# Which slot a tile gets, and the order of the steps of a layer's first chunk and of the convolution, in a one-core RWKV and graph-convolution kernel

## The chip, the cores and the metric

The kernel runs on one core of a Trainium2 chip. The metric is the device time of one execution in microseconds (us); lower is better. Five engines work side by side, each through its own list of instructions in order: PE (TensorE, matrix products into PSUM), DVE (VectorE), ACT (ScalarE), POOL (GpSimd), and SP, which here only issues DMAs. A semaphore makes an instruction wait for another engine; everything behind it in its list waits with it.

## The reference, cut to what matters

The input is x, 16 images of 192 channels by 56 by 56 positions (T = 3136). Three WKV layers, each added to its input, are followed by one graph convolution, also added.

```
per WKV layer:  xs = groupnorm(x) as [T, C];  k, v, r = xs Wk', xs Wv', xs Wr'
   forward  y_t = (p + e^(u+k_t) v_t) / (q + e^(u+k_t));  p <- e^w p + e^k v;  q <- e^w q + e^k
   backward the same from the other end;  h = sigmoid(r) * (y_fwd + y_bwd) / 2
   h = layernorm over channels(h);  x = x + h Wo'
convolution:  xn = groupnorm(x);  xj = max(0, the four shifts of xn by 2 rows or columns - xn)
   x = x + gelu([xn, xj] W' + b)
```

## The kernel before, in words

**Tiling.** Two images make a pair (8 pairs). A pair's 192 channels lie as three planes j = 0, 1, 2 of 128 partitions (plane 1 holds the last 64 channels of both images); `ORDER` is (0, 2, 1). T is cut into 7 chunks of L = 448 positions. A chunk's tile is 128 x 3 x 448 float32, a **slot**: there are 33 (`NSLOTS`), and `free` lists the free ones. `Slot(what)` takes the first of the list, `give()` puts one at its end. A slot's new writer waits for its old readers.

**Work per chunk.** A forward unit "A" (functions `a_*`): product k, exp (ek), product v, `a_ekv` (DVE, ekv = v ek), prefix scans `a_q` of ek and `a_p` of ekv (`scan`, DVE, three planes each), `a_den` and `a_num` (`bonus`, DVE), `invert` (ACT: Ln, then Exp of its negative), `a_y` (POOL, y = num times 1/den). `save` copies a scan's last column to the next chunk's tile. A backward unit "B" (`b_*`) runs the chunks from 6 to 0: product r (`b_gate`) and `b_exp`, scans `b_q` and `b_p`, `b_den`, `invert`, `b_num`, `b_sigmoid` (ACT), and `b_mix` (POOL, three operations per plane, nine in all: ekv times 1/den; added to the forward y; times the sigmoid). Then the layernorm: `b_squares` (ACT), `b_sums` (PE), `b_rs1` (ACT), `b_rs2` (PE), `b_rs3` (ACT), `b_spread` (PE, broadcast of 1/std, tile rsb), `b_scale` (DVE), product `b_out`, `b_x` (DVE, residual; wrapped by `add`, followed by a DMA to DRAM), and `b_stats` (ACT, sums for the next groupnorm, wrapped by `sum_up`). A convolution unit "C": product with half 0 of the weights (`c_product(a, 0)`), the maxima `c_rows` and `c_columns` (DVE), product with half 1, `c_gelu` (ACT, with a table load on each side), `c_add` (POOL), and `store` (DMA to the output).

**Steps.** Nothing is scheduled by a planner: under `manual_schedule` each engine's list is the order in which Python calls the operations. A list of 249 steps pairs the backward unit of one pair of images with a forward or convolution unit of another. `both_a_first` is the step of chunk A0 of a layer beside B5 (17 of them, each behind `backward_alone`), `both_a` the other steps of B and A (85), `both_c` those of B and C (42, in 7 groups of six; B runs from 5 to 0 and C from 0 to 5), `forward_a` an A alone (66), `forward_c` a C alone. `late` holds for each unfinished B how far its layernorm has come: of_stage(0) is the B of the step before, whose layernorm runs in this step; `gap()` runs one part of the groupnorm of a layer that is about to begin (`norm_sums`, `norm_var`, `norm_fold`, `norm_fold_r`). PSUM has seven banks for products (`banks` takes three, `release` gives them back).

**The two parts that change.** In `both_a_first` the order around the scan is

```
        a_q(*a) ... keys(nfront)
        a_p(*a, V)                 # the scan of ekv, then the save by DVE
        spread_and_scale(l)        # b_spread, b_scale, b_out of the B before
        ... a_den(*a); ln(den()); add(l); a_num(*a); exp_minus(den()); a_y(*a)
```

In `both_c`, inside a group, DVE's list is b_den, add, c_rows, c_columns, b_num, then the next B's b_q and b_p, then b_scale; PE's is gate r, cv half 0, sums, b_rs2, cv half 1, spread, out; ACT's is exp of r, squares, Ln, rs1, Exp, six statistics, rs3, sigmoid, gelu; POOL's is nine of b_mix, the save of p, c_add.

Of the kernel before, what the change touches and what calls it, by code (L numbers as in the profile page):

```python
# [473 lines left out]
def fast_path(ctx: ExitStack, tc: tile.TileContext, flag, x, wproj, wfold, wcfold, wconst, wgroup, sums, picks, vecs, out):  # L474
# [24 lines left out]

    free = [f"slot{i}" for i in range(NSLOTS)]  # L500

    class Slot:
        def __init__(self, what):
            self.tag = free.pop(0)
            rows = keep.tile([P, 3, L + 4], F32, tag=self.tag, name=name(what))
            self.full, self.lead = rows[:, :, 2 : L + 3], rows[:, :, 1 : L + 2]
            self.t = rows[:, :, 2 : L + 2]

        def give(self):
            free.append(self.tag)  # L510

# [347 lines left out]
    def scan(run, key, data, step, first):  # L859

        dec = params[run.l][0]
        s = Slot(key)
        for j in ORDER:
            if first:
                out, e = s.t[:, j, ::step], data.t[:, j, ::step]
            elif step > 0:
                out, e = s.lead[:, j, :], data.lead[:, j, :]
            else:
                out, e = s.full[:, j, ::-1], data.full[:, j, ::-1]
            V.tensor_tensor_scan(  # L870
                out, dec[:, column(j)].to_broadcast([P, L if first else L + 1]), e, 0.0, ALU.mult, ALU.add
            )
        return s
# [15 lines left out]

    def slot_of(slots, c, what):  # L890
        if c not in slots:
            slots[c] = Slot(what)
        return slots[c]
# [8 lines left out]
    def a_keys(run, c):  # L902
        if not once(run, "k", c):
            return
        product(run, "k", run.w[0], run.xa[c], c == 0)
        slot_of(run.ek, c, "ek")
        if c == 0:
            take_bias(run, "k", S)
# [42 lines left out]
    def a_p(run, c, eng=G):  # L951
        run.h[c] = scan(run, "p", run.ekv[c], AHEAD, c == 0)
        if c < NL - 1:
            save(run.h[c], AHEAD, slot_of(run.ekv, c + 1, "ekv"), eng)

# [19 lines left out]
    def a_y(run, c):  # L975
        den = run.den.pop(c)
        G.tensor_mul(run.h[c].t, run.h[c].t, den.t)  # L977
        den.give()

# [27 lines left out]
    def b_den(run, c):  # L1007
        q = run.q.pop(c)
        bonus(run, run.ek[c], run.ek[c], q)
        q.give()  # L1010

# [6 lines left out]
    def b_num(run, c):  # L1018
        p = run.p.pop(c)
        bonus(run, run.ekv[c], run.ekv[c], p)  # L1020
        p.give()

    def b_mix(run, c):
        y, h, sg, den = run.ekv.pop(c), run.h[c], run.sg.pop(c), run.ek[c]
        for j in ORDER:
            G.tensor_mul(y.t[:, j, :], y.t[:, j, :], den.t[:, j, :])  # L1026
            G.tensor_add(h.t[:, j, :], h.t[:, j, :], y.t[:, j, :])  # L1027
            G.tensor_mul(h.t[:, j, :], h.t[:, j, :], sg.t[:, j, :])  # L1028
        y.give()
        sg.give()  # L1030

# [5 lines left out]
    def b_sums(run, c):  # L1037
# [5 lines left out]
        for n, (t, i) in enumerate(parts):  # L1043
            PE.matmul(st[32 * n : 32 * n + 32, :L], ones[:, 1 + i, :], t[:, 1, :], start=False, stop=n < 2)  # L1044
        sq.give()

# [27 lines left out]
    def b_out(run, c):  # L1074
        h = run.h.pop(c)
        run.ps["o"] = banks("ops")
        project(run.ps["o"], params[run.l][5], of(h.t), L)
        h.give()

# [294 lines left out]
    def both_a_first(b, a, nback, nfront, loads):  # L1374
# [13 lines left out]
        b_mix(*b)  # L1388
        slot_of(a[0].ekv, a[1] + 1, "ekv")
        for u in loads:  # L1390
# [12 lines left out]
        keys(nfront)  # L1403
        a_p(*a, V)
        spread_and_scale(l)
# [6 lines left out]
        b_rs1(*b)  # L1412
        ln(den())
        add(l)
        a_num(*a)
        late[b] = 0.5
        exp_minus(den())
        a_y(*a)

    def both_c(b, a, nback, nfront, loads):  # L1420

        l0, l1, l2 = of_stage(0), of_stage(1), of_stage(2)
        load_ahead(nback)
        first = nback is not None and not l1
        b_q(*b)
        b_p(*b)
        if first:

            b_gate(*nback[1:])
            b_exp(*nback[1:])  # L1430
            c_product(*a, 0)
        if l0:
            squares_and_sums(l0)
        b_den(*b)
        ln(b[0].ek[b[1]])
        if l0:
            b_rs1(*l0)
        exp_minus(b[0].ek[b[1]])
        if l2:
            add(l2)  # L1440
            sum_up()
        if l1:
            spread_and_scale(l1)
        gap()
        store()
        for u in loads:
            load_ahead(u)
        if nback is not None:
            if not first:
                b_gate(*nback[1:])  # L1450
                b_exp(*nback[1:])
        else:
            keys(nfront)
            exp_keys(nfront)
        if not first:
# [12 lines left out]
        b_mix(*b)  # L1468
        if l1:
            add(l1)  # L1470
            sum_up()
        if nback is not None:
            b_q(*nback[1:])
            b_p(*nback[1:])
        ahead = nback is None and l0 and nfront is not None and nfront[0] == "A"
        if ahead:
            a_q(*nfront[1:])
            a_save(*nfront[1:])
            b_spread(*l0)
            c_end(*a, False)  # L1480
            a_values(*nfront[1:])
            b_scale(*l0)
            b_out(*l0)
            late[l0] = 2
        elif l0:
            spread_and_scale(l0)
        if not ahead:
            c_end(*a, False)
        late[b] = 0
# [201 lines left out]
    with tc.manual_schedule(engines={PE.engine, V.engine, S.engine, G.engine, nc.sync.engine}):  # L1691
# [46 lines left out]
        store()  # L1738
        assert not late and not unsummed and not convs

# [99 lines left out]
```

## Time and profile before

| what | us |
|---|---|
| median of 3 runs (5244.23 to 5249.13) | 5248.44 |
| profiled execution, its own time | 5246.37 |
| its span, from the first to the last instruction | 5244.4 |
| DVE busy (92%) | 4837.0 |
| PE busy (90%) | 4701.2 |
| ACT busy (70%) | 3680.4 |
| POOL busy (55%) | 2900.0 |
| mean granted PE clock | 0.943 |

A profile's row gives line, engine, operation, tiles out<-in, count, then busy time, mean ns of one, and the engine's idle time just before with what ended it. A timeline row gives start, duration, engine, line, operation and, in brackets, the idle time before and its releaser. Tile names are those of the code with numbers left out: in the rows of `b_mix` tile p is the forward y. "Busy" on DVE and POOL includes time in which an instruction has begun and is held up. A matmul's end is modelled, so PE's busy share is no measure of how near it is to its peak.

### The profile page before, as it was taken

The numbers are of one execution on the slowest core, as the hardware profiler recorded it, in microseconds if no ns is written. First come the engines' busy times: TensorE is split into PE (matmuls) and PEld (weight loads), VectorE is DVE, ScalarE is ACT, GpSimd is POOL, SyncE is SP. The second block draws the span as 40 slices with busy tenths as digits, with TensorE's granted clock in tenths as the row PEclk, the third lists the DMA queues.
The fourth block names the chain that finished last, engine by engine and source line by source line (L and its number), as shares of the span: only waits on it lengthen the run. The fifth ranks groups of instructions, "written<-read, shape, count | busy, mean of one in ns | idle before, by whom it ended". The sixth has DMA issues, their size and how long they took to land. (4 is left out here: it accounts for less than half of the span.)

```text
span 5244.4 us, 51899 instructions
## 1 busy us (share of the span) xinstructions
PE 4701.2 (90%) x15542; PEld 1493.0 (28%) x15542; DVE 4837.0 (92%) x6288; ACT 3680.4 (70%) x7163; POOL 2900.0 (55%) x2234
## 2 busy tenths in 40 slices
PE   7999998989899998898989999889898999999887
PEld 3222222223232222222323222222232322222222
DVE  6999889899999998999999999889999999999996
ACT  6777777776566777776656678778766667777672
POOL 1666555555455655555454556556545455666562
PEclk9999999999999999999999999999999999999998
DMA  5222222223232222223323223222332322222233
GB/s 153 69 82 82 95 82 92 85 90 116 89 116 71 87 90 88 85 85 100 118 79 113 84 74 100 87 78 93 115 100 87 111 74 76 75 83 81 73 108 114
DMA packets 314275, 482.47 MB, mean 92 GB/s; under 512 B 66432, under 2 KB 306688, under 8 KB 313984
## 3 DMA queue, kind: packets, MB, share of 16 engines
q1 hardware_dynamic: 312832, 477.59, 28.5%
q8 instruction: 125, 2.05, 0.2%
q10 hardware_dynamic: 1152, 1.48, 0.1%
q14 instruction: 166, 1.36, 0.1%
HBM read 324.83 MB, written 154.14 MB: 91 GB/s over the span
## 5 line engine op out<-in xcount | busy, mean ns | idle before, releaser
L870 DVE TENSOR_TENSOR_SCAN p<-fdecays,ekv 128x449 f32<-128x449 f32 (+1 forms) x1008 | 1021.9, 1069 | 113.8 <-POOL p L1027 60.1
L870 DVE TENSOR_TENSOR_SCAN q<-fdecays,ek 128x449 f32<-128x449 f32 (+1 forms) x1008 | 1024.7, 1072 | 8.9 <-ACT ek L915 8.8
L977 POOL TENSOR_TENSOR p<-p,q 128x1344 f32<-128x1344 f32 x168 | 511.6, 3045 | 838.2 <-ACT q L973 543.0
L1026 POOL TENSOR_TENSOR ekv<-ekv,ek 128x448 f32<-128x448 f32 x504 | 627.1, 1244 | 625.0 <-ACT ek L973 392.9
L1028 POOL TENSOR_TENSOR p<-p,sg 128x448 f32<-128x448 f32 x504 | 633.3, 1257 | 144.5 <-ACT ek L879 101.3
L1027 POOL TENSOR_TENSOR p<-p,ekv 128x448 f32<-128x448 f32 x504 | 600.9, 1192 | 39.5
L881 POOL COPY ekv<-p 128x3 f32<-128x3 f32 x265 | 221.8, 837 | 538.5 <-DVE p L870 531.5
L915 ACT ACTIVATE ek<-k,k 128x448 f32<-128x448 f32 x504 | 296.9, 633 | 213.1 <-PE k L596 168.1
L730 ACT ACTIVATE fjunk<-x 128x448 f32<-128x448 f32 x672 | 387.7, 577 | 39.4 <-DVE x L1084 13.0
L1035 ACT ACTIVATE ek<-p 128x448 f32<-128x448 f32 x504 | 279.4, 572 | 168.4 <-POOL p L1028 167.9
L1066 PE MATMUL rsb<-rs,fpicks 32*128 32x448 f32 (+1 forms) x1008 | 342.0, 602 | 46.8 <-ACT rs L1060 46.8
L991 ACT ACTIVATE sg<-r,r 128x448 f32<-128x448 f32 x504 | 313.1, 627 | 95.6 <-PE r L596 72.3
L885 DVE SCALAR_TENSOR_TENSOR ek<-ek,fcc,q 128x896 f32<-128x896 f32 x336 | 374.0, 1154 | 0.0
L1071 DVE TENSOR_TENSOR p<-p,rsb 128x448 f32<-128x448 f32 x504 | 281.7, 615 | 92.0 <-PE rsb L1066 92.0
L1084 DVE SCALAR_TENSOR_TENSOR x<-ops,fwob,x 128x448 f32<-128x448 f32 x504 | 315.6, 674 | 49.3 <-PE ops L596 30.2
L729 ACT ACTIVATE fjunk<-x 128x448 f32<-128x448 f32 x600 | 342.8, 571 | 11.4
L885 DVE SCALAR_TENSOR_TENSOR q<-ek,fcc,q 128x896 f32<-128x896 f32 x336 | 343.0, 1062 | 6.3 <-ACT cvb L949 4.6
L1050 ACT ACTIVATE rs<-st 64x448 f32<-64x448 f32 x168 | 90.2, 537 | 358.0 <-PE st L1044 358.0
L970 ACT ACTIVATE q<-q 128x1344 f32<-128x1344 f32 x168 | 221.7, 1319 | 162.1 <-DVE q L885 114.1
L593 PE MATMUL ops<-p,fwo 128*128 128x448 f32 x336 | 210.0, 713 | 139.6 <-DVE p L1071 139.3
L935 DVE SCALAR_TENSOR_TENSOR ekv<-v,v,ek 128x448 f32<-128x448 f32 x504 | 313.5, 676 | 11.9 <-PE v L602 5.7
L885 DVE SCALAR_TENSOR_TENSOR ekv<-ekv,fcc,p 128x896 f32<-128x896 f32 x336 | 322.2, 1000 | 0.0
(236 smaller groups left out, 11827.6 us busy)
## 6 DMA issues: line engine op xcount, KB each, us to landing
x<-xd SPq DMA_DIRECT2D x240, 672.0 KB, 5.2
xd<-x SPq DMA_DIRECT2D x168, 672.0 KB, 3.8
x<-in_x_dram SPq DMA_DIRECT2D x320, 224.0 KB, 4.1
x<-in_x_dram SPq DMA_DIRECT2D x320, 112.0 KB, 4.0
out_dram<-ml SPq DMA_DIRECT2D x112, 224.0 KB, 2.3
m<-xd SPq DMA_DIRECT2D x112, 168.0 KB, 4.8
wkv<-in_wfold_dram SPq DMA_DIRECT2D x24, 640.0 KB, 5.4
out_dram<-ml SPq DMA_DIRECT2D x112, 112.0 KB, 2.3
```

Source lines behind the costliest of these rows:

```text
L729: S.activation(junk, xt[:, j, :], AF.Identity, accum_out=stats[:, 0, j, c : c + 1])
L730: S.activation(junk, xt[:, j, :], AF.Square, accum_out=stats[:, 1, j, c : c + 1])
L870: V.tensor_tensor_scan(out, dec[:, column(j)].to_broadcast([P, L if first else L + 1]), e, 0.0, ALU.mult, ALU.add)
L885: by_channel(lambda js, i: V.scalar_tensor_tensor(dst.t[:, js, :], e.t[:, js, :], cc[:, i : i + 1], state.t[:, js, :], ALU.mult, ALU.add))
L935: V.scalar_tensor_tensor(e.t[:, j, :], ps[j][:, 0:L], b[:, j, :], run.ek[c].t[:, j, :], ALU.add, ALU.mult)
L977: G.tensor_mul(run.h[c].t, run.h[c].t, den.t)
L991: S.activation(sg.t[:, j, :], ps[j][:, 0:L], AF.Exp, bias=b[:, j, :], scale=-1.0, accum_out=run.chk[:, at : at + 1])
L1026: G.tensor_mul(y.t[:, j, :], y.t[:, j, :], den.t[:, j, :])
L1027: G.tensor_add(h.t[:, j, :], h.t[:, j, :], y.t[:, j, :])
L1028: G.tensor_mul(h.t[:, j, :], h.t[:, j, :], sg.t[:, j, :])
L1066: PE.matmul(ps[j][:, :L], pick[rows, j, :], rs[rows, :], start=True, stop=True)
L1084: V.scalar_tensor_tensor(xj, ps[j][:, 0:L], wob[:, column(j)], xj, ALU.add, ALU.add, accum_out=run.new[:, 0, j, c : c + 1] if c == 0 else ...
```

## The change

Three things are done, all by reordering or by choosing another buffer. No arithmetic operation is added or removed; one kind of small copy moves from DVE to POOL.

1. `free` keeps with each slot the engine that read it last. A taker may name an engine: it then gets a slot last read by that engine if there is one, else one not last read by DVE, else any. Scans name DVE, ek names PE, ekv names the engine of its save.
2. `both_a_first`: the save after `a_p` goes to POOL, its slot is no longer taken early, and `invert` and `a_num` come ahead of `add`.
3. `both_c`: `b_scale` comes ahead of the next B's scans, `add` ahead of `b_den`; `b_spread` follows `b_gate`; the second half of a chunk's convolution product, its gelu and `c_add` are done in the following step; `b_out` opens the following step; the statistics go between the squares; Ln and Exp stand together ahead of `b_rs1`; the three `gap()` calls stand after `b_rs3`, after `c_rows` and after `c_columns`. In the last step of a group the current chunk's second product is done in the step itself, beside the one carried over.

```diff
-    free = [f"slot{i}" for i in range(NSLOTS)]
+    free = [(f"slot{i}", None) for i in range(NSLOTS)]
     class Slot:
-        def __init__(self, what):
-            self.tag = free.pop(0)
+        def __init__(self, what, engine=None):
+            own = [slot for slot in free if engine is not None and slot[1] is engine]
+            slot = (own + [slot for slot in free if slot[1] is not V] + free)[0]
+            free.remove(slot)
+            self.tag = slot[0]
...
-        def give(self):
-            free.append(self.tag)
+        def give(self, engine=None):
+            free.append((self.tag, engine))
...
-        s = Slot(key)
+        s = Slot(key, V)                                  (scan)
-        slot_of(run.ek, c, "ek")
+        slot_of(run.ek, c, "ek", PE)                      (a_keys)
-            save(run.h[c], AHEAD, slot_of(run.ekv, c + 1, "ekv"), eng)
+            save(run.h[c], AHEAD, slot_of(run.ekv, c + 1, "ekv", eng), eng)
                  den.give(G); q.give(V); p.give(V); y.give(G); sg.give(G); sq.give(PE); h.give(PE)
both_a_first:
-        slot_of(a[0].ekv, a[1] + 1, "ekv")
...
-        a_p(*a, V)
+        a_p(*a)
...
-        ln(den())
+        late[b] = 0.5
+        invert(den())
+        a_num(*a)
         add(l)
-        a_num(*a)
-        late[b] = 0.5
-        exp_minus(den())
         a_y(*a)
+    half = []
both_c:
-        l0, l1, l2 = of_stage(0), of_stage(1), of_stage(2)
+        l0, l1 = of_stage(0), of_stage(1.5)
         load_ahead(nback)
         first = nback is not None and not l1
+        store()
         b_q(*b)
         b_p(*b)
+        if l1:
+            b_out(*l1)
         if first:
             b_gate(*nback[1:])
             b_exp(*nback[1:])
             c_product(*a, 0)
+        if half:
+            c_product(*half[0], 1)
         if l0:
-            squares_and_sums(l0)
+            b_squares(*l0, (0,))
+        sum_up()
+        if l0:
+            b_squares(*l0, (2, 1))
+            b_sums(*l0)
+        if l1:
+            add(l1)
         b_den(*b)
-        ln(b[0].ek[b[1]])
+        invert(b[0].ek[b[1]])
         if l0:
             b_rs1(*l0)
-        exp_minus(b[0].ek[b[1]])
-        if l2:
-            add(l2)
-            sum_up()
-        if l1:
-            spread_and_scale(l1)
+            b_rs2(*l0)
+            b_rs3(*l0)
         gap()
-        store()
+        if half:
+            u = half.pop()
+            c_gelu(*u, False)
+            c_add(*u)
         (loads; keys, or b_gate and b_exp where not first, as before)
+        if l0:
+            b_spread(*l0)
         if not first:
             c_product(*a, 0)
         c_rows(*a)
-        if l0:
-            b_rs2(*l0)
-            b_rs3(*l0)
-            late[l0] = 1
+        gap()
         c_columns(*a)
-        c_product(*a, 1)
-        gap()
         gap()
         b_num(*b)
         b_sigmoid(*b)
         b_mix(*b)
         if nback is not None:
+            if l0:
+                b_scale(*l0)
+                late[l0] = 1.5
             b_q(*nback[1:])
             b_p(*nback[1:])
-        (spread_and_scale(l0) and c_end(a), or with the next A's start between them)
+            half.append(a)
+        else:
+            (a_q and a_save of the next A where it is one; c_product(a, 1); c_end(a);
+             a_values of that A; b_scale(l0), b_out(l0), late[l0] = 2)
         late[b] = 0
```

More of the change, by code (lines that the diff above doesn't have):

```diff
@@ L861, in scan @@
         dec = params[run.l][0]
-        s = Slot(key)
+        s = Slot(key, V)
         for j in ORDER:
@@ L888, in fast_path, with slot_of @@
     AHEAD, BACK = 1, -1
-    def slot_of(slots, c, what):
+    def slot_of(slots, c, what, engine=None):
         if c not in slots:
-            slots[c] = Slot(what)
+            slots[c] = Slot(what, engine)
         return slots[c]
@@ L905, in a_keys @@
         product(run, "k", run.w[0], run.xa[c], c == 0)
-        slot_of(run.ek, c, "ek")
+        slot_of(run.ek, c, "ek", PE)
         if c == 0:
@@ L977, in a_y @@
         G.tensor_mul(run.h[c].t, run.h[c].t, den.t)
-        den.give()
+        den.give(G)
     def b_gate(run, c):
@@ L1009, in b_den @@
         bonus(run, run.ek[c], run.ek[c], q)
-        q.give()
+        q.give(V)
     def b_p(run, c):
@@ L1020, in b_num @@
         bonus(run, run.ekv[c], run.ekv[c], p)
-        p.give()
+        p.give(V)
     def b_mix(run, c):
@@ L1028, in b_mix @@
             G.tensor_mul(h.t[:, j, :], h.t[:, j, :], sg.t[:, j, :])
-        y.give()
-        sg.give()
+        y.give(G)
+        sg.give(G)
     def b_squares(run, c, js=ORDER):
@@ L1044, in b_sums @@
             PE.matmul(st[32 * n : 32 * n + 32, :L], ones[:, 1 + i, :], t[:, 1, :], start=False, stop=n < 2)
-        sq.give()
+        sq.give(PE)
     def b_rs1(run, c):
@@ L1077, in b_out @@
         project(run.ps["o"], params[run.l][5], of(h.t), L)
-        h.give()
+        h.give(PE)
     def b_x(run, c):
@@ L1431, in both_c @@
             c_product(*a, 0)
+        if half:
+            c_product(*half[0], 1)
         if l0:
-            squares_and_sums(l0)
+            b_squares(*l0, (0,))
[5 more added lines that the diff above has]
+            add(l1)
         b_den(*b)
-        ln(b[0].ek[b[1]])
+        invert(b[0].ek[b[1]])
         if l0:
             b_rs1(*l0)
-        exp_minus(b[0].ek[b[1]])
-        if l2:
-            add(l2)
-            sum_up()
-        if l1:
-            spread_and_scale(l1)
+            b_rs2(*l0)
+            b_rs3(*l0)
         gap()
-        store()
+        if half:
+            u = half.pop()
+            c_gelu(*u, False)
+            c_add(*u)
         for u in loads:
             load_ahead(u)
[L1448 to L1452, printed above, removed]
+        if nback is None:
             keys(nfront)
             exp_keys(nfront)
+        elif not first:
+            b_gate(*nback[1:])
+            b_exp(*nback[1:])
+        if l0:
+            b_spread(*l0)
         if not first:
@@ L1468, in both_c @@
         b_mix(*b)
-        if l1:
-            add(l1)
-            sum_up()
         if nback is not None:
+            if l0:
+                b_scale(*l0)
+                late[l0] = 1.5
             b_q(*nback[1:])
             b_p(*nback[1:])
[L1475 to L1479, printed above, removed]
-            c_end(*a, False)
[L1481 to L1488, printed above, removed]
+            half.append(a)
+        else:
+            ahead = nfront is not None and nfront[0] == "A"
+            if ahead:
+                a_q(*nfront[1:])
+                a_save(*nfront[1:])
+            c_product(*a, 1)
+            c_end(*a, False)
+            if ahead:
+                a_values(*nfront[1:])
+            if l0:
+                b_scale(*l0)
+                b_out(*l0)
+                late[l0] = 2
         late[b] = 0
@@ L1738, in fast_path @@
         store()
-        assert not late and not unsummed and not convs
+        assert not late and not unsummed and not convs and not half
     least = small.tile([P, 1], F32, tag="p2", name="fleast")
```

## The prediction

> **What bounds the kernel now.** I read the page's busy shares first, then who waited for whom on DVE, then time windows of single steps, then timelines inside them.
>
> ```profile
> PE 4701.2 (90%) x15542; PEld 1493.0 (28%) x15542; DVE 4837.0 (92%) x6288; ACT 3680.4 (70%) x7163; POOL 2900.0 (55%) x2234
> ...
> DVE p L1071 <- PE rsb L1066: 92.0, 54, 18.6
> DVE p L870 <- POOL p L1027: 60.1, 18, 6.8
> DVE p L870 <- POOL p L1028: 53.6, 6, 9.0
> DVE x L1084 <- PE ops L596: 30.2, 22, 4.4
> ```
>
> DVE and PE are both near full, so a wait of DVE costs time unless PE is behind as well. The second and third wait (columns: total, times, longest) are of a scan for POOL, and the data of that scan come from DVE itself. L1027 and L1028 are the last readers of two slots that `b_mix` frees: the scan waits for its output buffer, 113.7 us in 24 places.
>
> Windows of one step each (time, then busy of PE, PEld, DVE, ACT, POOL, granted clock), for one pair of layers with these waits and one without:
>
> ```profile
> 712.80:751.40 38.60, 34.09 (x119) 10.64 (x118) 26.05 (x35) 21.94 (x42) 18.85 (x16) 0.91 0.18 56
> ...
> 1645.60:1673.70 28.10, 27.44 (x107) 8.58 (x106) 26.28 (x35) 18.90 (x34) 17.90 (x15) 1.00 0.23 75
> ...
> 1721.80:1745.40 23.60, 23.30 (x82) 7.11 (x80) 23.60 (x30) 19.29 (x38) 15.22 (x12) 1.00 0.27 89
> ```
>
> The first two rows run from `both_a_first` to the step behind it: DVE's work is equal (26.1 and 26.3), the time is 38.6 against 28.1. The third is a `both_a` step without a wait: DVE full at 23.6, PE right behind it. Inside the slow one:
>
> ```profile
> 730.21 3.05 DVE L870 TENSOR_TENSOR_SCAN p<-fdecays,ekv 128x448 f32<-128x448 f32 x3 [8.95 <-POOL p L1028]
> 733.29 0.17 DVE L881 COPY ekv<-p 128x3 f32<-128x3 f32 x1
> ...
> 739.22 1.28 DVE L1084 SCALAR_TENSOR_TENSOR x<-ops,fwob,x 128x448 f32<-128x448 f32 x2 [2.52 <-PE ops L596]
> 741.55 0.69 DVE L1084 SCALAR_TENSOR_TENSOR x<-ops,fwob,x 128x448 f32<-128x448 f32 x1 [1.05 <-PE ops L602]
> ...
> 728.22 1.97 PE L1066 MATMUL rsb<-rs,fpicks 32*128 32x448 f32 x6
> ...
> 729.04 1.13 POOL L1028 TENSOR_TENSOR p<-p,sg 128x448 f32<-128x448 f32 x1
> ```
>
> The scan could start at 721.2; it starts when `b_mix` ends. What would stop DVE next is the PE row: rsb, which starts at 728.2.
>
> Convolution steps, by windows:
>
> ```profile
> 1138.30:1166.60 28.30, 23.85 (x86) 7.27 (x82) 27.27 (x31) 22.49 (x42) 16.09 (x11) 1.00 0.24 81
> 1166.60:1191.50 24.90, 24.10 (x80) 7.63 (x80) 24.83 (x32) 16.64 (x30) 15.76 (x11) 0.93 0.44 137
> 1191.50:1223.20 31.70, 29.03 (x105) 10.24 (x104) 28.08 (x42) 24.72 (x51) 16.05 (x11) 0.95 0.53 174
> ...
> 1159.29 3.42 POOL L1154 TENSOR_TENSOR ml<-ml,x 128x1344 f32<-128x1344 f32 x1
> ...
> 1159.70 3.04 DVE L1121 TENSOR_TENSOR ml<-x 128x16 f32<-128x16 f32 x1
> ```
>
> DVE looks full, but the last row is an operation on 16 elements (0.16 to 0.17 us elsewhere) that takes 3.04 us while `c_add` runs on POOL: some of DVE's busy time is being held up.
>
> **Part 1, slots.** By the rule of the change a forward scan gets the slot that `b_den` or `b_num` of the same step has just freed, last read by DVE itself, in all 102 steps of B and A. So all 24 waits go. What each is worth depends on what is late next.
> - Six first steps with about 9.0 us. By the timeline: scan 721.2 to 724.2; rsb's first plane is ready about 729.1, so DVE waits there 4.9; scaling to 730.8, a_den to 732.5, a_num to 734.2, add to 736.1. Before, the same work ended at 743.8. Gain 7.7, the reordering of part 2 included.
> - Three first steps with 6.8 (at 538): rsb comes at 537.7 there; the same sum ends at 544.5 instead of 549.95. Gain 5.5.
> - Fifteen later steps: the rest, 113.7 - 53.6 - 20.5 = 39.6. DVE is the bound there (PE's 22.7 us of work against 23.6), so I take it whole.
> - Waits on rsb that follow a slot wait one step later (2.0 and 0.6 us, in six groups, together 7.9): PE fell behind because `b_scale` came late. Gone too; bounds 0 and 7.9, I take 7.9.
>
> Sum: 6 x 7.7 + 3 x 5.5 + 39.6 + 7.9 = 110. The slots that other users get instead are a risk that the trace doesn't show: loads and `b_exp` could wait for `b_mix`. Bounds 0 and 9.0 us a step (the longest wait of this kind now); nothing lower, as a wait can't give time. I take 0, because those users write a step later and `b_mix` is done some 10 us before.
>
> **Part 2, the first step.** In the eight first steps without a slot wait `add` waits 0.26 + 0.59 for PE (at 1661.7); behind a_num it no longer does: 0.8 each, 6. The save moves to POOL: 0.42 us of DVE (x17, L881), hidden under the wait for rsb, against a POOL copy of 0.84 mean (x265, L881) between `b_mix` and `a_y`, where POOL idles 16 us (746.5). Both at nothing; without that cover 0.4 each way.
>
> **Part 3, the convolution.** I work out what one step needs on three paths, from uncontended rows.
> - PE: four products of 4.5 (r from 1179.34 to 1183.84), rsb 1.97, sums 1.75, rs2 0.96: 22.7.
> - DVE: scaling 1.6, scans 5.9, add 1.8, b_den 1.7, rows 1.6, columns 5.7, b_num 1.7: 20.0.
> - A loop through ACT and POOL, which the new order closes. From the last POOL operation of `b_mix`: last square 0.6, Ln and Exp 2.6, rs1 0.5, rs2 1.1, rs3 1.3, then gelu with its two table loads 4.5, three exps of r 2.1, sigmoid 2.7 (Ln at 1170.09, next free at 1172.8), and the seven `b_mix` operations that need the sigmoid, 8.2: 23.6. Before, gelu stood behind the sigmoid and was no part of such a loop.
>
> The shared port. The row above shows DVE held for the whole of `c_add`. The Trainium skill, SBUF — State Buffer, "Who interferes with whom", states why: a DVE instruction with two SBUF inputs and a GpSimd one that reads SBUF exclude each other for the whole instruction, while one SBUF input contends with nothing. By that rule scaling, scans and add (one input is PSUM) are free beside `b_mix`, and b_den, rows, columns, b_num are not. In the new order the nine operations of `b_mix` lie beside scaling, scans and add, 9.3 us; only b_den (two of 0.83) meets the last three. `c_add` comes 9.4 us behind the end of `b_mix`, when columns are over (they end at about 7). So the held-up time on DVE goes, but DVE no longer sets the step: POOL loses about 1.2 to b_den, and the loop becomes 23.6 + 1.2 = 24.8; I take 25.0.
>
> The clock. PE gets half its clock now and then: after the 2.2 us of waiting ahead of 1166.7 the window 1166.7 to 1170.1 shows 0.51 granted. The skill, TensorE: Matmul & The Clock Gate, "What's actually happening", says the clock halves after about 3.4 us of an idle window and a busy window releases it. By the trace shorter waits can do it. This speaks against the change: PE now waits for the sums (some 2 us) and for rs2 (1.5) in each step. By the rule neither halves it, PE stays at 22.7 and the loop at 25.0 holds; by the trace one window of 3.4 a step costs 1.7, PE 24.4, still under 25.0. The sum is the same; a second window would break it (below).
>
> Group by group: the first convolution step is as before up to the end of b5's mix (1128.4). Then four loops of 25.0, plus 3.0 where a groupnorm falls in (table scale 1.7 and rstd now ahead of the sigmoid; DVE's 3.3 of waiting for rstd moves behind c_rows), put the last mix's end at 1231.4. The last step carries two second products, 4.5 more on PE, and b_out of the one before: from 4.8 behind that end PE has k, rsb, cv, cv, v, 20.0, plus 1.0 for half clock: 1257.2 for the end of v, for which DVE waits. Now v ends at 1260.2. Gain 3 in six groups, and 5 in the last (no groupnorm, no v): 23. The new wait on v (about 5 us of DVE) is in this.
>
> SP: `store` moves to the head of the step, ahead of add's DMA; the four DMAs wait only for a `c_add` issued half a step earlier, and loads are a step ahead; 0, bounds 0 and 2.3 (a store's time to landing) a step for the one tile in six whose slot is written in that step.
>
> Sum: 110 + 6 + 23 = 139 off the profiled execution's 5246.4: 5107. The median lies 2.1 above that execution: **5110**. This kernel's measurement tells about 0.2% from no change.
>
> **The rivals.**
> - *Main case*, 0.50: 5110, own range 5070 to 5150.
> - *The convolution falls to PE's 22.7*: the loop is shorter than I think (the last three of `b_mix` not held up, table loads ahead of gelu's wait). For it: PE idle 0.1 to 0.9 us in two of the windows. Against: the loop's rows. 35 x 2.3 = 80 more: 5030. 0.20.
> - *The slot waits come back*: the fifteen later ones turn into waits on rsb, and half of the first steps' gain goes to half clock; convolution even. 5246.4 - 55 - 6 + 2 = 5187. For it: the 92.0 us on rsb and 0.91 clock in the slow window. Against: the window of 23.6. 0.21.
> - *Slower*: two waits of PE in each convolution step keep it at half clock through gate r and, a step on, out. Each takes 9.0 instead of 4.5, exps of r come 3.2 late, the addition and b_den follow; the loop is 29.5. 35 x 4.5 = 158 on top, less the 23: 5246.4 - 116 + 135 + 2 = 5267. It decides from a loop of about 29 us. Against: windows of half clock are mostly 3.4 or 6.8 now. 0.06.
> - *Even*, a loop near 28.5: 0.03.
>
> Faster by over 0.2% is the first three, 0.91; within 0.2% 0.03; slower 0.06. The range 5030 to 5190 reaches to both neighbours of the main case and leaves out the last two and part of the second.
>
> **What would show it.** No wait of L870 p on POOL; in first steps one on rsb of about 5 us in its place; `both_a` steps at 23.6 to 24.5 everywhere. Convolution steps near 25 each with DVE below 22 busy, no 3 us operation of 16 elements, POOL waiting for the sigmoid, ACT's list without long gaps; one wait on v at a group's end. Wrong it would be if the scans wait for something else, if `c_add` still lies beside columns, or if a convolution step is over 28 or under 23.

## The result, and the profile after

Eight runs of the changed kernel have a median of 5221.5 us (5199.0 to 5223.1), eight of the kernel before 5248.6 us (5242.4 to 5253.3): ratio 0.9945, interval 0.9936 to 0.9954. The change brings 27 to 29 us where the prediction had 139. The profiled execution took 5220.2 us, its span is 5218.2.

The page's row of busy times, then what DVE waited for (total, times, longest):

```profile
PE 4733.3 (91%) x15542; PEld 1498.8 (29%) x15542; DVE 4750.5 (91%) x6271; ACT 3684.6 (71%) x7163; POOL 2889.2 (55%) x2251
...
DVE p L1076 <- PE rsb L1071: 194.4, 96, 20.7
DVE nm L749 <- PE psg L607: 33.6, 14, 4.6
DVE v L862 <- PE v L601: 32.9, 6, 5.5
...
DVE q L875 <- ACT ek L920: 25.4, 7, 7.9
...
DVE v L862 <- PE v L607: 10.5, 7, 1.6
```

No scan waits for POOL any more: 113.7 us are gone as forecast. But the wait for rsb has grown from 92.0 us in 54 places to 194.4 in 96, and three small waits are new. (Lines stand five lower than before: L1071 for rsb is L1076 here for the scaling that waits, the scan is L875.)

Windows of single steps (time, then busy of PE, PEld, DVE, ACT, POOL, granted clock): a first step; a later step with statistics of the other pair's input (`count(z)`); one without them; then four steps of a convolution group, the third with the groupnorm:

```profile
711.80:741.60 29.80, 29.14 (x112) 8.86 (x110) 26.42 (x34) 20.46 (x39) 18.95 (x17) 1.00 0.14 47
794.90:822.20 27.30, 24.89 (x81) 7.62 (x80) 24.62 (x30) 20.45 (x42) 15.65 (x12) 0.94 0.23 77
1671.20:1694.80 23.60, 23.31 (x82) 7.12 (x82) 23.60 (x31) 19.29 (x38) 15.34 (x13) 1.00 0.28 89
1128.10:1151.20 23.10, 21.32 (x77) 6.78 (x78) 21.46 (x32) 17.47 (x33) 15.47 (x11) 1.00 0.41 135
1151.20:1175.60 24.40, 22.63 (x82) 7.07 (x80) 21.36 (x31) 18.76 (x35) 15.05 (x11) 1.00 0.47 158
1175.60:1209.30 33.70, 31.92 (x116) 10.99 (x114) 25.79 (x42) 24.98 (x47) 18.09 (x12) 0.95 0.39 120
1209.30:1230.50 21.20, 18.14 (x59) 5.46 (x59) 21.13 (x31) 14.94 (x26) 15.66 (x12) 0.91 0.40 123
```

The first step fell from 38.6 to 29.8, and the convolution steps are short. The second row is what was not foreseen: no engine is full in it, and the clock is 0.94. In all nine groups with statistics the four later steps now run up to this length (26.4, 26.9, 27.1 and 27.2 in the first of them).

To see where the time went I cut the whole run into intervals, each from the start of `b_num` on DVE in one step to that of the next, and summed the differences to the kernel before by kind (us; "late" are the four intervals behind a first step, "C0–C4" and "C5" the first five and the last of a convolution group, which holds the forward steps behind it too). Later kernels are in the same table; its sums come from one profiled execution each. The interval ahead of a first step, within 1 us in every row, is left out, so a row adds up to its total within 2.

| kernel | first | late | A5 | C0–C4 | C5 | all |
|---|---|---|---|---|---|---|
| predicted | -69 | -47 | 0 | -23, with C5 | | -139 |
| changed | -73 | +43 | +2 | -54 | +58 | -26 |
| slots only | -10 | +31 | -5 | +3 | +3 | +20 |
| slots, no early ekv | -63 | +37 | -1 | +6 | +11 | -10 |
| slots and first step | -66 | +37 | -4 | +5 | +8 | -21 |
| convolution only | -18 | 0 | +7 | -53 | +41 | -24 |
| before, statistic moved | -8 | -46 | +2 | 0 | 0 | -51 |
| changed, statistic moved | -72 | -66 | +4 | -53 | +36 | -153 |
| changed, inversion first | -69 | -63 | +5 | -55 | +36 | -147 |
| changed, PE filled | -66 | 0 | +18 | -54 | +37 | -66 |

The first steps are right, the late ones are 91 off with the wrong sign, and the convolution is 27 off, as C5 gives back what C0 to C4 win.

### The profile page after: what moved, and what is told of

It reads as the page before. It is cut to its first block, busy times and chain, and to the rows that moved or that the text cites. A ratio compares the mean times of both kernels' runs of the same rounds, so it can differ in the third digit from the quotient of the medians.

```text
span 5218.2 us, 51856 instructions
## 1 busy us (share of the span) xinstructions
PE 4733.3 (91%) x15542; PEld 1498.8 (29%) x15542; DVE 4750.5 (91%) x6271; ACT 3684.6 (71%) x7163; POOL 2889.2 (55%) x2251
## 5 line engine op out<-in xcount | busy, mean ns | idle before, releaser
L875 DVE TENSOR_TENSOR_SCAN q<-fdecays,ek 128x449 f32<-128x449 f32 (+1 forms) x1008 | 1023.4, 1068 | 28.0 <-ACT ek L920 25.4
L875 DVE TENSOR_TENSOR_SCAN p<-fdecays,ekv 128x449 f32<-128x449 f32 (+1 forms) x1008 | 1020.3, 1065 | 0.6
L1031 POOL TENSOR_TENSOR ekv<-ekv,ek 128x448 f32<-128x448 f32 x504 | 602.7, 1196 | 456.1 <-ACT ek L978 385.3
L886 POOL COPY ekv<-p 128x3 f32<-128x3 f32 x282 | 233.1, 827 | 488.0 <-DVE p L875 457.2
L1076 DVE TENSOR_TENSOR p<-p,rsb 128x448 f32<-128x448 f32 x504 | 282.4, 613 | 194.5 <-PE rsb L1071 194.4
L1071 PE MATMUL rsb<-rs,fpicks 32*128 32x448 f32 (+1 forms) x1008 | 359.2, 629 | 42.4 <-ACT rs L1065 42.4
L1159 POOL TENSOR_TENSOR ml<-ml,x 128x1344 f32<-128x1344 f32 x56 | 178.9, 3194 | 391.8 <-ACT ml L1150 391.8
L890 DVE SCALAR_TENSOR_TENSOR q<-ek,fcc,q 128x896 f32<-128x896 f32 x336 | 359.2, 1109 | 6.3 <-ACT cvb L954 4.6
L996 ACT ACTIVATE sg<-r,r 128x448 f32<-128x448 f32 x504 | 313.0, 627 | 33.5 <-PE r L607 20.7
L890 DVE SCALAR_TENSOR_TENSOR p<-ekv,fcc,p 128x896 f32<-128x896 f32 x336 | 295.3, 919 | 6.5 <-POOL ekv L886 1.7
```

Of the source, the lines that this page charges most:

```text
L875: V.tensor_tensor_scan(out, dec[:, column(j)].to_broadcast([P, L if first else L + 1]), e, 0.0, ALU.mult, ALU.add)
L890: by_channel(lambda js, i: V.scalar_tensor_tensor(dst.t[:, js, :], e.t[:, js, :], cc[:, i : i + 1], state.t[:, js, :], ALU.mult, ALU.add))
L996: S.activation(sg.t[:, j, :], ps[j][:, 0:L], AF.Exp, bias=b[:, j, :], scale=-1.0, accum_out=run.chk[:, at : at + 1])
L1071: PE.matmul(ps[j][:, :L], pick[rows, j, :], rs[rows, :], start=True, stop=True)
```

## What one of the slow steps is made of

Timeline of the changed kernel from 799 to 829 (start, duration, engine, line, what, in brackets the idle time before it and what ended it):

```profile
799.23 1.68 DVE L1076 TENSOR_TENSOR p<-p,rsb 128x448 f32<-128x448 f32 x3 [2.60 <-PE rsb L1071]
800.86 1.15 POOL L1031 TENSOR_TENSOR ekv<-ekv,ek 128x448 f32<-128x448 f32 x1 [6.43 <-ACT ek L978]
812.47 0.95 PE L1049 MATMUL st<-p,fsums 128*32 128x448 f32 x4 [2.42 <-POOL p L1033]
814.37 1.86 PE L598 MATMUL r<-x,wr 128*128 128x448 f32 x2
820.22 0.63 ACT L996 ACTIVATE sg<-r,r 128x448 f32<-128x448 f32 x1 [0.53 <-PE r L607]
820.85 0.56 ACT L734 ACTIVATE fjunk<-x 128x448 f32<-128x448 f32 x1
...
825.50 1.97 PE L1071 MATMUL rsb<-rs,fpicks 32*128 32x448 f32 x6
...
828.18 1.15 POOL L1031 TENSOR_TENSOR ekv<-ekv,ek 128x448 f32<-128x448 f32 x1 [6.41 <-ACT ek L978]
```

This is a loop. `b_mix` starts on POOL at 800.86 and ends at 812.4. Its last square and the sums on PE take until 814.37; the gate's product r until the last exponential can start, 820.22; that ends at 820.85. Then ACT works off, in its order, the statistic (1.3), a small save and rs3 (1.5), the sigmoid (2.6), the inversion of two planes (2.0), and the next `b_mix` starts at 828.18. From 800.86 that is 27.3: 11.6 + 1.9 + 6.5 + 1.3 + 1.5 + 2.6 + 2.0, less what rounding adds. DVE's wait for rsb hangs from the same chain: once the sums can start, PE has no gap up to rsb at 825.50, which stands behind r, rs2 and v (rs3 on ACT was done at 823.6).

Two of these terms are longer than need be. The sums and r run behind PE's wait of 2.42 us, and PE is then at half clock. The same place 190 us earlier, in windows of 3.4 us:

```profile
618.90:622.30 3.40, 1.31 (x12) 0.24 (x6) 3.40 (x3) 0.87 (x2) 3.32 (x3) 1.00 0.30 114
622.30:625.70 3.40, 3.40 (x10) 1.03 (x7) 3.31 (x5) 1.59 (x3) 0.07 (x1) 0.50 0.05 9
625.70:629.10 3.40, 3.40 (x13) 0.99 (x11) 3.40 (x5) 2.97 (x6) 1.60 (x1) 0.99 0.60 198
```

PE is busy 1.31 of 3.40 us, and the next 3.4 us are granted at 0.50. At full clock sums and r take 1.5 and 4.5 (from 792.41 in the kernel with the statistic moved, below), 1.7 less. After the result I first took the loop as it stands, at 27.2, with half clock as a rival. From the run with the statistic moved on (below) the theory was: **a loop through POOL, PE and ACT of about 25.6 us, which PE's wait stretches to 27.3 by half clock.** Its rivals: PE, or ACT, or DVE sets these steps by its own work; or the clock only follows and the loop is 27.3 without it. In the kernel before, DVE's waits for slots stood in front of all this.

## Experiments: which part does what

**The slots alone.** The kernel before with the new `Slot`, `give` and their callers; first step and convolution as before.

> The kernel before with the rule for slots alone (first step and convolution steps in the old order). Loop theory: what the slots gain in first steps is mostly lost again in the steps behind them that carry input statistics, because those now settle at about 27.2 us by a loop through PE, ACT and POOL. Summing intervals of the two traces over the forward groups gave about -29 us, of it at most 6 from the first step's new order, so this kernel comes out 22 to 30 us under the kernel before (ratio 0.994 to 0.996). Rival, mine of the prediction (slots alone are worth about 110, and the new convolution order or the first step took it back): ratio about 0.979. Rival, the slots do nothing for the time by themselves: 1.000.

Measured: 5266.7 us, ratio 1.0047 (1.0033 to 1.0061): slower, outside all three. The late steps behave as in the changed kernel, but the first steps gained only 10, though no scan waits for POOL. What they wait for instead, on ACT, then on DVE:

```profile
729.36 0.64 ACT L996 ACTIVATE sg<-r,r 128x448 f32<-128x448 f32 x1 [6.21 <-POOL p L1032]
...
734.22 1.16 DVE L1076 TENSOR_TENSOR p<-p,rsb 128x448 f32<-128x448 f32 x2 [9.43 <-PE rsb L1071]
```

The exponentials of r write a new slot, and the only ones left were those that `b_mix` reads. rs3 stands behind them on ACT, rsb behind rs3, DVE's scaling behind rsb: 8.95 us of waiting for POOL became 9.43 of waiting for PE.

**The slots without the early ekv.** The same, and one line less.

```diff
 both_a_first:
-        slot_of(a[0].ekv, a[1] + 1, "ekv")
```

> The kernel with the rule for slots alone, and one line of both_a_first less: the early taking of the next ekv slot, which the change drops too. In the run with the line, the gate's exponentials of that step waited 6.2 us for b_mix in six first steps (their new slot was the one POOL still reads), rs3, rsb and DVE's scaling behind them, so the first steps took 39.1 us as before. Theory (it is this hand-out of slots that ate the first steps' gain): without the line the exponentials find another slot, the first steps fall to some 31 us, 55 to 65 off, the later steps with statistics lose 25 to 30 as in the changed kernel; together some -25 us to the kernel before, ratio 0.994 to 0.997. Rival (it is the new order of DVE's work in the first step that brings the gain, not the slots): first steps at 36 or more, ratio 1.000 to 1.005.

Measured: 5233.2 us, ratio 0.9975 (0.9966 to 0.9984). The first steps give -63, as the theory said, at 30.2 and 31.8 us; the gain of the first steps belongs to the slots and to this one line of the change, not to the order of DVE's work. It is a little less than expected in sum, as C5 lost 11.

**Slots and first step**, the changed kernel with the convolution of before.

> The changed kernel with the convolution steps of before: slots and first step together. Sums of intervals over the forward groups in the changed kernel: -29 us, ratio 0.9945. If the two halves of the change simply add (the convolution order alone measured 0.9951, both 0.9945), this kernel stands at 0.9994, -3 us. The prediction had -116, ratio 0.978.

Measured: 5232.6 us, ratio 0.9972 (0.9961 to 0.9984), between the two sums. Against the run before it the new order of the first step is worth nothing that can be measured.

**The convolution alone.** The kernel before with the new `both_c`.

> The kernel before with the new order of the convolution steps alone. Interval sums of the two traces say that the convolution groups won about 7 us each in their first five steps and lost 8 to 9 in the last one, with the norm step 1.5 longer: together about +3 us, ratio 0.999 to 1.002. The prediction's sum: -23 us, ratio 0.9956. Rival, the loss of the last step comes from the slots and not from the order: then this kernel keeps the gain of 7 a group, about -40 us, ratio 0.992.

Measured: 5218.9 us, ratio 0.9951 (0.9938 to 0.9965), -24 us. That is outside the +3 that I expected from the intervals. It is the prediction's -23, but not made as it said: C0 to C4 win 53, C5 loses 41, and the first and A5 intervals of other groups, most of them with no convolution before them, moved by -11 together. What moved those was not tried.

## Experiments: what sets the late steps

**Statistic moved.** One edit on the changed kernel, in `both_a`:

```diff
-        count(z)
         b_q(*b)
...
             exp_minus(b[0].ek[b[1]], js)
+        count(z)
         b_num(*b)
```

> The changed kernel with one edit: in both_a the first of the two input statistics of a step (two ACT passes of 0.57 with their reads of the sum, 1.46 us) is issued behind the inversion that b_mix waits for, instead of between the gate's exponentials and rs3. Loop theory (b_mix, squares, sums, gate, exponentials, statistics, rs3, sigmoid, inversion, b_mix): the loop is shorter by about 1.4, the 36 steps with statistics go from 27.2 to about 25.8, some 50 us under the changed kernel: ratio to the kernel before about 0.985. Rival, PE is what sets these steps (its waits bring half clock whatever ACT does): they stay near 27.2, ratio 0.9945 as the changed kernel. Rival, ACT is simply full in these steps: no change either, and ACT would show no idle time.

Measured: 5100.2 us, ratio 0.9732 (0.9718 to 0.9745): 121 us under the changed kernel by the medians, 112 by the ratios, for two ACT passes (1.3 us) taken out of the loop in each step with statistics. The direction is the loop's, the size is over twice what a plain loop gives. A step of it in windows, and PE's wait in it from the timeline:

```profile
779.70:803.20 23.50, 23.18 (x82) 7.11 (x80) 23.50 (x30) 20.41 (x42) 15.32 (x12) 1.00 0.26 88
...
792.41 0.95 PE L1049 MATMUL st<-p,fsums 128*32 128x448 f32 x4 [0.32 <-POOL p L1033]
```

PE waits 0.32 instead of 2.42, the clock is 1.00, and DVE is full at 23.5: these steps are at last what the prediction took them for.

Half clock does not make up the whole difference; a third term does. In the changed kernel's slow step the last operation of `b_mix` on POOL and `a_den` on DVE hold each other up:

```profile
810.30 2.60 DVE L890 SCALAR_TENSOR_TENSOR q<-ek,fcc,q 128x896 f32<-128x896 f32 x2
...
810.40 2.02 POOL L1033 TENSOR_TENSOR p<-p,sg 128x448 f32<-128x448 f32 x1
```

With the statistic moved `b_mix` ends before `a_den` starts:

```profile
791.21 1.15 POOL L1033 TENSOR_TENSOR p<-p,sg 128x448 f32<-128x448 f32 x1
...
792.39 1.74 DVE L890 SCALAR_TENSOR_TENSOR q<-ek,fcc,q 128x896 f32<-128x896 f32 x2
```

The traces show the hold-up in all 36 late steps with statistics of the changed kernel, and in none with the statistic moved. So the loop loses 1.3 for the statistic, 1.7 for half clock and 0.9 on POOL: 27.3 becomes 23.4, and DVE's 23.6 is left as the bound.

**Inversion ahead of the sigmoid** (of the two outer planes), another way to shorten the same loop:

```diff
-        b_sigmoid(*b)
...
             exp_minus(b[0].ek[b[1]], js)
+            if js is AC:
+                b_sigmoid(*b)
```

> The changed kernel with one edit: in both_a ACT inverts the denominator's two outer planes ahead of the gate's sigmoid, which only b_mix's third operation needs. Loop theory: b_mix starts 2.6 us earlier and is then held up 0.4 for the sigmoid, so the loop is shorter by about 2.2: steps with statistics at about 25.0, some 36 x 2.2 = 80 us under the changed kernel, ratio to the kernel before about 0.979; steps without statistics, bound by DVE at 23.6, stay. Rival, PE sets the steps: ratio 0.9945, and b_mix's end moves earlier with nothing else following.

Measured: 5097.4 us, ratio 0.9718 (0.9705 to 0.9731), 119 under the changed kernel by the ratios. Two different cuts in the loop give the same, as DVE is the bound behind both; here too the hold-up is gone from all 36 steps.

**Statistic moved in the kernel before**, with its old slots:

> The kernel before, old slots and all, with the one edit that gave 121 us on the changed kernel: the step's first input statistic behind the inversion. Theory (the slot waits and the loop through ACT stand one behind the other, and the one hid the other): alone the edit only ends b_mix some 1.4 us sooner, and so shortens the slot waits by up to that: 24 waits x 1.4 = 34 at most, ratio 0.993 to 0.998. Rival (the edit is worth its 121 us by itself and the slots nothing): ratio 0.977. Rival (nothing, the slot waits hold all): 1.000.

Measured: 5197.9 us, ratio 0.9908 (0.9892 to 0.9923), -48. More than the slot waits could give: those on L870 fell by 17.7, with those for rsb and ops it is 27, and DVE's busy time by another 21 (in the kernel before `a_den` is held up in 21 late steps, here in none). So the loop already cost something before the change, beside the slot waits. By the ratios the change is worth 29, the moved statistic 48, the two together 141: each had covered the other's gain.

**Useless ACT passes in the steps that have no statistic**, to make the loop longer where it had done no harm. With n = 1, 2, 3:

```diff
 both_a:
+        if not z:
+            for _ in range(n):
+                S.activation(junk[:, 0 : 3 * P], pick.rearrange("p j c -> p (j c)"), AF.Identity)
         count(z)
```

> The changed kernel with a useless ACT pass (128x384, about 0.5 us) in those both_a steps that carry no statistic, at the place where the others have theirs, ahead of rs3. These steps (four a group in eight groups) ran at 23.6, bound by DVE. Theory of the loop with clock: PE's wait for the last sums is 0.29 there; it grows by the pass, to under 1 us, which does not halve the clock, so the loop still closes within 23.6 or a little over: steps 23.6 to 24.0, +0 to 15 us. Rival, a loop with no part of the clock: also 23.6 up to its slack. Rival, ACT's filling is no cause at all: no change at any dose.

> The same with two passes, about 1.0 us. Loop with clock: if PE's wait for the sums reaches that of the slow steps (2.1 us, half clock behind it), the step jumps to about 27.3 at once, +3.7 each, some +120 us; if not, it is at most 24.1. Rival, a plain loop: the step grows by what the dose exceeds its slack, 23.6 to 24.6, at most +32 us.

> The same with three passes, about 1.5 us, as much as one input statistic. Loop with clock: these steps become what the steps with statistics are, 27.2 to 27.3, with windows of half clock 27.3 apart and DVE waiting about 2 us for rsb in each; some +120 us to the changed kernel, ratio to before about 1.017. Rival, a plain loop: 23.6 to 25.1, +48 at most. Rival, PE or ACT as a whole set the slow steps: 23.6, as ACT has room.

A pass takes 0.52 us. The same late step of the second group (23.60 without a pass), one pass, then two, then three, in windows; for two and three with PE's wait for the sums:

```profile
423.10:447.00 23.90, 23.22 (x82) 7.07 (x82) 23.82 (x30) 19.62 (x39) 15.28 (x12) 1.00 0.27 86
```

```profile
425.40:449.90 24.50, 23.27 (x82) 7.12 (x82) 24.42 (x31) 20.07 (x40) 15.27 (x12) 1.00 0.26 84
...
439.23 0.95 PE L1049 MATMUL st<-p,fsums 128*32 128x448 f32 x4 [1.23 <-POOL p L1033]
```

```profile
438.00:465.20 27.20, 24.70 (x82) 7.47 (x82) 25.10 (x31) 20.66 (x41) 15.49 (x12) 0.94 0.24 76
...
455.03 1.43 PE L1049 MATMUL st<-p,fsums 128*32 128x448 f32 x4 [2.50 <-POOL p L1033]
```

The first pass costs 0.3, the second 0.6, the third 2.7. A plain loop would have gone to about 25.1. At three passes the clock falls to 0.94, the last operation of `b_mix` takes 1.86 (at 453.12), and the step is that of the groups with statistics to a tenth. In time: 5213.5 us (0.9940, 0.9922 to 0.9958), 5239.2 (0.9988, 0.9981 to 0.9995), 5300.8 (1.0107, 1.0088 to 1.0125). That is +79 at three passes where +120 was expected: by the intervals each of the eight groups loses 11 to 12 instead of 15, since the steps take two or three to reach 27.3 (26.4, 27.1, 27.2, 27.3 in the second group).

**Work added on PE.** If half clock is a cause, keeping PE busy in its wait must shorten the steps with statistics, although nothing is taken out of the loop. With n = 2 and 4, in those steps only:

```diff
 b_sums:
+        for _ in range(n):
+            PE.matmul(st[:, 0 : 3 * P], pick[:, 0, :], pick.rearrange("p j c -> p (j c)"), start=True, stop=True)
```

> The changed kernel with useless work added on PE: two products of 128x384 (about 0.9 us) ahead of the sums in the both_a steps with statistics, in the place where PE waits 2.09 us for b_mix and then runs at half clock. Nothing is taken away from ACT's list. Theory that half clock is part of the 27.3 (a plain loop would close at about 25.5): the wait that PE has left is 1.2, and if that is too short to halve the clock, the steps fall to 25.4 to 25.7 though they hold more work, 27 to 36 steps x 1.7 = 45 to 60 us under the changed kernel, ratio 0.983 to 0.986. Rival (the clock only follows, the loop alone makes 27.3): no change, ratio 0.9945, or slower by what the added work does not fit.

> The same with four such products, about 1.7 us: PE is left with 0.4 of waiting at the old pace, and at the pace of 25.5 with none, so up to 1.3 of the added work may come to stand in the loop. Half clock as part of the loop: 25.5 to 26.5 a step, ratio 0.984 to 0.992. Rival: 27.3 or more, ratio 0.9945 or above.

A step with n = 2 in windows, then the added products and PE's wait behind them:

```profile
793.40:819.00 25.60, 24.67 (x85) 7.71 (x85) 24.55 (x30) 20.27 (x42) 15.71 (x12) 1.00 0.25 85
...
805.93 1.56 PE L1046 MATMUL st<-fpicks 128*128 128x384 f32 x4
...
809.31 0.95 PE L1051 MATMUL st<-p,fsums 128*32 128x448 f32 x4 [0.93 <-POOL p L1033]
```

Measured: 5191.4 us with two (0.9903, 0.9888 to 0.9918) and 5208.5 with four (0.9933, 0.9918 to 0.9948). The late steps are 25.4 to 25.7 in both, as expected: more work, and 1.6 us less per step. Half clock is a cause and not a companion, and 25.6 is the loop without it (the hold-up on POOL, 2.05 at 807.20, is still in it). (The two products are four instructions, 1.56 us instead of the 0.9 that I had reckoned.) The sum for n = 2 is 22 by the ratios and 30 by the medians, not 45 to 60, because A5 gave back 16, and 40 with four products; there, it seems, the added work counts. (The table's row for n = 2 is of an execution that lies 13 us under the median.)

## Experiments: what sets the convolution's last step

**v ahead of the second product, groupnorm's sums ahead of b_den**, on the kernel with the statistic moved:

```diff
 both_c:
-        gap()                       (behind b_rs3)
+        gap()                       (ahead of b_den)
         b_den(*b)
...
+            if l0:
+                b_scale(*l0)
+            if ahead:
+                a_values(*nfront[1:])
             c_product(*a, 1)
             c_end(*a, False)
-            if ahead:
-                a_values(*nfront[1:])
```

> The changed kernel with the statistic behind the inversion (ratio 0.973 by itself) and two edits in the convolution. First, the groupnorm's sums are issued ahead of b_den, so that their small products on PE stand ahead of rs2: DVE waited 4.6 us for them in six groups; expected C3 intervals 33.5 to about 30, 20 us. Second, in a group's last step PE makes v ahead of the second half of the convolution: DVE waited 5.5 + 1.6 for v in six groups (five to six have that form); expected 4.5 a group, 20 to 25 us, unless gelu, now 4.5 later on ACT, holds up the next step's squares as long. Together ratio 0.965 if both hold, 0.973 if PE sets these steps and the waits only move.

Measured: 5100.3 us, ratio 0.9723 (0.9710 to 0.9736), no different from the statistic alone. The norm step did fall, from about 33.5 to between 31.2 and 32.3. In C5 the wait for v of 5.54 is down to 1.03, but 12 us later DVE waits as long for a save on ACT, which stands behind the gelu that now comes later:

```profile
1220.95 1.75 DVE L890 SCALAR_TENSOR_TENSOR p<-ekv,fcc,p 128x896 f32<-128x896 f32 x2 [5.86 <-ACT ekv L884]
```

PE has no gap from 1199 to 1226 in that timeline, as it should be if C5 is PE's.

**Groupnorm's sums alone**, on the same kernel: the first of the two edits.

> The changed kernel with the statistic behind the inversion and the groupnorm's sums ahead of b_den, without the inversion's new place, which in the kernel with all three put the sigmoid behind a wait of ACT for b_den and cost 29 us. Norm intervals 33.5 to 31.3 in five groups, -10 at most; against that PE is behind in the group's last step, which took the same sum back in two runs. Ratio 0.970 to 0.973; 0.973 if the last step gives it all back.

Measured: 5118.6 us, ratio 0.9761 (0.9747 to 0.9774), slower than without. C0 to C4 win 66 instead of 53, C5 loses 63 instead of 36. The run before this one differs from it only by the new place of v and `b_scale`, and is 20 us faster by the ratios, with C5 at +48: beside this edit the order in C5 does count. The traces show 16.5 us at half clock in each of the six C5 here, 6 to 14 there.

**All three**: statistic moved, inversion first, groupnorm's sums.

> The changed kernel with three edits that held up singly: the statistic behind the inversion, the inversion's outer planes ahead of the sigmoid, and the groupnorm's sums ahead of b_den. The first two cure the same loop and steps with statistics already stand at DVE's 23.6, so they do not add: 145 to 150 off the kernel before, plus some 2 in each of five norm steps: ratio 0.970 to 0.972. Rival: the norm steps' gain goes into the group's last step, where PE is behind anyway: 0.972 to 0.973.

Measured: 5129.0 us, ratio 0.9777 (0.9763 to 0.9790), 24 to 31 worse by the ratios than either of the first two edits alone. Every second late step is 25.0 instead of 23.6, where ACT waits for `b_den` at the head of the inversion, with the sigmoid behind it:

```profile
807.49 0.95 ACT L975 ACTIVATE ek<-ek 128x896 f32<-128x896 f32 x1 [2.53 <-DVE ek L890]
```

and C5 loses 60. The best of all are the two single edits, 2.7 to 2.8% under the kernel before.

## Why the prediction was right or wrong

**Slots, first steps: right** in size (-73 for -69), with the wait on rsb in their place (2.55 us at 726.63 where the prediction had 4.9). The reordering inside that sum was given 6 and is worth nothing measurable.

**The slots of the others: priced at 0, which held by luck.** The prediction bounded this risk by 0 and 9.0 a step and took 0 because "those users write a step later". The slots-only kernel shows the other bound: 6.2 us on ACT in six first steps. The dropped line for ekv, which the prediction does not mention, takes those six away.

**Slots, later steps: the step that failed.** "Fifteen later steps: … DVE is the bound there (PE's 22.7 us of work against 23.6), so I take it whole", and the 7.9 on rsb beside it: -47.5 forecast, +43 measured. The 23.6 came from the window 1721.80:1745.40, which lies in a group without statistics, while the waits lay in groups with them. There the engines' loads say little. What the runs show in place of DVE as the bound is the loop through POOL, PE and ACT: 25.6 at full clock, longer than the work of any engine, and 27.3 with half clock, so that the waits for slots came back as waits for rsb (194.4 us for 92.0). The prediction drew such a loop for the convolution and not for the steps next to it, where ACT carries 1.3 us more ahead of the sigmoid. It also let DVE and POOL meet in `b_den` of the convolution and priced that at 1.2, but not here, where `a_den` and `b_mix` meet for 0.9. Its second rival, slot waits that come back as waits on rsb, named what happened and put 55 + 6 on what would be left of the gain; for these steps it is what should have been likeliest.

**The clock.** The prediction weighed the rule only in the convolution. The Trainium skill, TensorE: Matmul & The Clock Gate, "What's actually happening", has half clock begin after at least one idle window of about 3.4 us. By that rule a wait of 2.4 costs itself and no more, and these steps would be 25.6. Here a window with PE busy 1.31 of 3.40 us is followed by half clock, and waits of 0.93 and 1.23 in the filled and the two-pass kernel are not. The measurement decides, as the prediction had half seen in its own trace: what counts is a poorly filled window, not an empty one. Cut on the clock's own steps of 3.41 us, the changed kernel's trace from 140 us on has 62 windows at full clock with PE busy for less than 0.40 of them, and half clock follows every one; from 0.40 to 0.62 it follows 49 of 77, above that 7 of 1159. The wait makes half clock, half clock lengthens the gate's product, that delays the next `b_mix`, and so PE's next wait: the step keeps itself slow.

**Convolution: the mechanism half right, the sum by chance.** The held-up operations are gone, as forecast; in the timelines of DVE and POOL the 16-element maximum and `c_add`, now apart:

```profile
1146.46 0.16 DVE L1126 TENSOR_TENSOR ml<-x 128x16 f32<-128x16 f32 x1
```

```profile
1153.73 3.04 POOL L1159 TENSOR_TENSOR ml<-ml,x 128x1344 f32<-128x1344 f32 x1 [8.49 <-ACT ml L1150]
```

DVE is at 21.4 in these steps (under 22, as said). But T was mis-sized: 23.1 and 24.4 measured for 25.0, and 21.2 in C4; which row of the loop was too long was not worked out. The norm step is 33.7 for 28.0, as DVE waits for the groupnorm's sums, which stand behind rs2 on PE; the prediction had moved the wait for rstd and has none for the sums:

```profile
1199.61 0.16 DVE L749 TENSOR_SCALAR nm<-psg 128x3 f32<-128x3 f32 x1 [4.64 <-PE psg L607]
```

And the last step was taken as 5 us of waiting for v:

```profile
1248.81 0.23 DVE L862 COPY v<-v 128x1 f32<-128x1 f32 x2 [5.54 <-PE v L601]
```

That wait is there, but C5 is 8 to 9.5 longer in six groups. Some 4.5 of that, by the prediction's 4.5 for a product, is the product carried over from the step before, as it reckoned: it leaves C0 to C4 and comes back in C5, so that part of their win is only moved. The rest goes along with the clock, for which the prediction added 1.0. C5 of the third convolution group before, changed, and with the statistic moved:

```profile
2817.90:2935.10 117.20, 108.87 (x346) 35.24 (x346) 110.89 (x151) 59.37 (x96) 46.81 (x29) 0.97 0.29 85
```

```profile
2795.80:2920.90 125.10, 117.94 (x364) 37.92 (x362) 110.23 (x151) 66.86 (x116) 48.79 (x30) 0.94 0.28 84
```

```profile
2717.00:2837.60 120.60, 111.97 (x360) 36.08 (x358) 109.55 (x151) 66.77 (x116) 48.74 (x30) 0.99 0.29 87
```

PE is at half clock for 6.8, 14.5 and 3.4 us of them. Where C0 to C4 became shorter still (-65), C5 gave it all back or more (+48 to +63, from +36). That fits PE as the bound over the whole group, with DVE only running ahead in the short steps, but no run shows it.

**What is open.** With its code unchanged, C5 is between 120.6 and 127.5 from group to group and from kernel to kernel (six groups; the last is longer). In 54 such intervals, of nine kernels, the length goes with the time at half clock: 120.6 at 3.4 us of it, 127.5 at 16.7, and 0.40 us longer for each microsecond between (correlation 0.86). No run changed the clock in C5 alone, so cause and consequence are not told apart there.

## What to carry to other kernels

Take the step that is to become the new bound from the same stage and with the same load as the wait that is removed; a window of a neighbouring group without the statistics promised 23.6 where the loop gave 25.6, and 27.3 with half clock. Behind a removed wait, look for loops across engines before engine loads, by following one buffer round until it comes back: two passes of 1.3 us together inside such a loop, moved to the other side of the operation that closes it, were worth more here than the whole change. Look in such a loop for terms that come and go with its length, here half clock (1.7) and two operations that meet (0.9): they made a cut of 1.3 worth 3.7 a step. And when slots are handed out by a rule, look who gets those that the rule's users no longer take.

## What was not expected of the hardware

Half clock can lock onto a loop. The granted clock changes in steps of 3.41 us; in the slow groups the windows of half clock are 27.3 us apart, eight of these, and the step is 27.3. With PE kept busy in its wait it goes to 25.6, with 1.3 us less in the loop to 23.6; two added products on PE made the kernel faster by 22 to 30 us.

The changed kernel's time comes in more than one size: mostly 5220.2 to 5223.1, but also 5213.7 and 5199.0, the shorter ones with a higher granted clock (0.944 at 5199.0, 0.940 at 5213.7, 0.935 at 5220.2). The kernel with two passes spread from 5219.9 to 5250.0; in its trace one group with statistics stands at 25.7 and the others end at about 27.3, with the same code. So a loop near the point where the clock tips can fall on either side.
